# A graph-attention layer on one core: node logits added and weights turned by TensorE, five tiles of every batch fetched by columns

## The chip, the cores and the metric

The kernel runs on one core of one Trainium2 chip. The metric is the device time of one execution in microseconds (us). The profile of one execution is read beside it. Engines are named as in the profile: PE is TensorE, PEld its weight loads, DVE is VectorE, ACT is ScalarE, POOL is GpSimd and SP is SyncE.

## The reference: what is computed

12500 nodes have 128 features, 412500 edges (sorted by target) have 64. Node rows are normalised, cut at zero and projected; every edge gets a logit for each of 4 heads, a leaky step, a softmax over the edges of its target, and the weighted source rows are summed for each target. Cut to what matters:

```python
h = jnp.maximum(_layernorm(x), 0.0)
h = (h @ W_node.T).reshape(num_nodes, H, HD)            # H = 4 heads, HD = 32
e = (edge_attr_64 @ W_edge.T).reshape(num_edges, H, HD)
att = jnp.sum(jnp.concatenate([h[src], h[tgt], e], -1) * a, -1)
att = jnp.where(att > 0, att, 0.2 * att)
m = jnp.maximum(segment_max(att, tgt), 0.0)
ex = jnp.exp(att - m[tgt])
denom = segment_sum(ex, tgt) + (num_edges - deg)[:, None] * jnp.exp(-m)
out = x + segment_sum((ex / denom[tgt])[:, :, None] * h[src], tgt)
```

## The kernel before

A lead-in of some 300 us writes a table of projected node rows (576 B each) to HBM and keeps the normalised node features, turned, in SBUF as `features`. Then come 66 batches. A batch holds 7 chunks of 7 tiles of 128 edges, so 49 tiles; its source rows stand in one of three buffers `hs` (RING = 3).

**Three ways a tile of source rows arrives.** Most tiles come by one indirect gather on POOL each (`gather_tile`, L334). One tile comes row by row, by single DMAs of SP (`row_by_row`, L864). A few tiles come by columns: the 128 source numbers are loaded as registers, 32 at a time, and 32 copies of one column of `features` each (128x1) put them side by side in `turned`; PE projects the tile with the weights `wall` and ACT copies it into `hs` (`put_back`, L904/L905). Such a set of one register load (L852) and 32 copies is called a group here; a tile is four groups. Before, the batches take three and four tiles by columns in turn, and the ones with three also a quarter of the tile that comes by rows (L909/L911), so 13 and 16 groups.

**Who does the groups.** `OF_SCALAR` and `OF_VECTOR` say how many groups ACT (L885) and DVE (L883) do in a batch, of even and of odd number; the batch whose tiles they prepare is two ahead or more. `BEHIND` lists the places in DVE's program where one group may stand; a batch uses the first few of the list. ACT does two groups at fixed places among the work after the exponentials, two more where a merge stands, and what is left of its number at the end of the batch, ahead of the next exponentials.

**A batch b, in program order** (`weigh`, `mark`, `scatter`, `choose`, `close`). The order is written out by hand; each engine goes through its own list in that order.
- POOL: a memset `gate` (L819) waits for the last matmul that reads the buffer to be filled (`scatter` of batch b - 2, L1095), then the gathers of batch b + 1 follow.
- SP: the rows of batch b + 2 with its edge features `eft` between them (L760).
- DVE: `weigh` copies the source logits out of `hs` (L1000), turns them in 32x32 blocks (L1001), adds them to PE's logits `z` in four steps (L1004), does the leaky step (L1007, L1008), two scans for the maximum of each target (L1009, L1012) and a subtraction (L1014). ACT takes the exponential in four steps (L1016), DVE masks the maxima in four (L1018), turns both in one instruction into PSUM (L1021) and copies the maxima into `hs` (L1026). `mark` builds the one-hot matrices `hot` (L951 to L958), `scatter` multiplies the rows by their weights in two pieces (L1089), and PE sums them with 14 matmuls into `pa` (L1095). They may start when ACT has copied the sums of the batch before out of `pa` (`collect`, L1120).
- After that DVE compares targets (`choose`, L789), every second batch DVE and ACT merge two batches' sums into `acc`, and PE begins the logits of batch b + 2 (`begin`, L935 and L938).

Of the kernel before, what the change touches and what calls it, by code (L numbers as in the profile page):

```python
# [9 lines left out]
F32 = mybir.dt.float32  # L10
# [13 lines left out]
H = 4  # L24
# [135 lines left out]
def kernel(  # L160
# [195 lines left out]
    with (  # L356
# [140 lines left out]
        def of_vector(u):  # L497
            return (u.s.b0 + u.i0) // XS % 3 == 0 and u.m == XS
# [228 lines left out]
    bank = ps.tile([P, 2 * T * R + W + GB * 4], F32, name="exr")  # L727
    both_ps = bank[:, :2 * T * R].rearrange("p (w t r) -> p w t r", w=2, t=T)
    ex_ps = both_ps[:, 0, :, :]
    rows_ps = bank[:, 2 * T * R:2 * T * R + W]  # L730
# [252 lines left out]
    def open_weights(s):  # L983

        s.zst = work.tile([P, T, R], F32, name="zst")
# [3 lines left out]
        s.both = work.tile([P, 2, T, R], F32, name="both")  # L989

    def weigh_part(s, t0, t1):

        zst, att, up, m, both = s.zst, s.att, s.up, s.m, s.both
# [3 lines left out]
        def grouped(what, g):  # L997
            return what.rearrange("r (t g i) -> r g t i", g=NQT, i=R)[:, g, t0:t1, :]
# [9 lines left out]
        on_half(s, nc.vector.tensor_tensor(z, up[:, e0:e1], att[:, e0:e1], op=OP.max))  # L1008
# [3 lines left out]
        nc.vector.tensor_tensor_scan(mp[:, ::-1], s.pen[:, e1:e0:-1], up[:, e0:e1][:, ::-1], 0.0, op0=OP.add, op1=OP.max)  # L1012
        of_vector("down")
        on_half(s, nc.vector.tensor_tensor(att[:, e0:e1], z, mp, op=OP.subtract))  # L1014
        for g in range(NQT):
            nc.scalar.activation(both[g * R:(g + 1) * R, 0, t0:t1, :], grouped(att, g), AF.Exp)  # L1016
        for g in range(NQT):
            nc.vector.scalar_tensor_tensor(both[g * R:(g + 1) * R, 1, t0:t1, :], grouped(s.pen[:, 1:], g), -1.0 / BIG,  # L1018
                                           grouped(up, g), op0=OP.mult, op1=OP.mult)
        if t1 - t0 == T:  # L1020
            nc.vector.transpose(both_ps.rearrange("p w t r -> p (w t r)"), both.rearrange("p w t r -> p (w t r)"))  # L1021
        else:
            for w in range(2):
                nc.vector.transpose(both_ps[:, w, t0:t1, :].rearrange("p t r -> p (t r)"),  # L1024
                                    both[:, w, t0:t1, :].rearrange("p t r -> p (t r)"))
        nc.vector.tensor_copy(own, both_ps[:, 1, t0:t1, :s.chunks * H].rearrange("p t (q h) -> p t q h", h=H))  # L1026

# [279 lines left out]
    with tc.manual_schedule():  # L1307
# [20 lines left out]
        for b in range(NBT - 1):  # L1328
# [28 lines left out]
            if later:  # L1357
                put_back(later, 0)
            if b < NBT - 2:
                mark(s)  # L1360
            for store in stores:
# [340 lines left out]
```

## Time and profile before

| what | value |
|---|---|
| time, median of 3 runs | 6768.51 us (6765.73 to 6787.56) |
| the profiled execution: its own time, its span | 6719.83 us, 6718.1 us |
| PE, PEld busy | 1803.4 us (27%), 724.3 us (11%) |
| DVE busy | 2718.8 us (40%), 13514 instructions |
| ACT busy | 2583.9 us (38%), 20492 instructions |
| POOL busy | 2797.8 us (42%), 3018 instructions |
| gathers from the table | 2887, 947 ns each |
| column copies on ACT, on DVE | 18624 (187 ns), 9888 (142 ns) |

No engine is busy for half of the span. Register loads and waits count as idle time, so a group costs more than its copies' busy time; idle time with the word "issue" is time in which an engine waited for nothing that the profile shows.

### The profile page before, as it was taken

How to read it: one execution, taken by the hardware profiler on the slowest of the kernel's cores; microseconds unless marked ns; L12 is line 12 of the kernel's file. 1: busy time of each engine (PE TensorE's matmuls, PEld its weight loads, DVE VectorE, ACT ScalarE, POOL GpSimd, SP SyncE). 2: the span in 40 equal slices, each digit the busy share in tenths (PEclk: the TensorE clock that was granted, in tenths of full speed). 3: DMA queues.
4: the chain of work that ended last, by engine and by line, in shares of the span. 5: the costliest groups of instructions: out<-in, count | busy, mean ns of one | idle time of the engine just before them, and what ended most of it. 6: DMA issues, size and time to landing. Idle time of an engine off the chain costs nothing. (4 is left out here: it accounts for less than half of the span.)

```text
span 6718.1 us, 65140 instructions
## 1 busy us (share of the span) xinstructions
PE 1803.4 (27%) x4569; PEld 724.3 (11%) x4569; DVE 2718.8 (40%) x13514; ACT 2583.9 (38%) x20492; POOL 2797.8 (42%) x3018
## 2 busy tenths in 40 slices
PE   4223123223123232222232232133123223312323
PEld 3101001011011011010011011011011001101111
DVE  4434334344344243353343344344334334434445
ACT  4134334334344344344344344344334434433420
POOL 4453443343443443533533443443453353344351
PEclk8566566566566566665666566566566566656666
DMA  4322222222222222222222222222222222222221
GB/s 115 94 61 58 61 61 64 61 61 62 57 63 65 59 64 60 64 65 57 64 66 61 65 66 61 62 63 61 67 64 65 59 61 67 62 66 65 64 66 43
DMA packets 225620, 432.22 MB, mean 64 GB/s; under 512 B 92316, under 2 KB 125094, under 8 KB 225144
## 3 DMA queue, kind: packets, MB, share of 16 engines
q0 software_dynamic: 94240, 216.84, 13.5%
q1 hardware_dynamic: 100664, 145.09, 7.4%
q10 hardware_dynamic: 30240, 66.08, 2.8%
q14 instruction: 438, 3.59, 0.2%
q8 instruction: 38, 0.62, 0.0%
HBM read 412.21 MB, written 15.53 MB: 64 GB/s over the span
## 5 line engine op out<-in xcount | busy, mean ns | idle before, releaser
L885 ACT COPY turned<-features 128x1 f32 x18624 | 2053.1, 187 | 3473.0 <-issue 3469.9
L334 POOL DMA_INDIRECT hs<-table,ends x2887 | 2734.6, 947 | 1006.8 <-issue 895.0
L819 POOL MEMSET gate<- 128x1 f32 x63 | 6.2, 99 | 2758.7 <-PE pa L1095 2751.6
L1095 PE MATMUL pa<-hs,hot 128*128 128x504 f32 x1820 | 937.0, 680 | 531.5 <-ACT r L1120 478.6
L904 PE MATMUL more<-wall,turned 128*128 128x144 f32 x430 | 155.5, 457 | 3011.5 <-ACT hs L905 2985.0
L883 DVE COPY turned<-features 128x1 f32 x9888 | 681.8, 142 | 691.9 <-issue 689.8
L1021 DVE STREAM_TRANSPOSE exr<-both 128x448 f32<-128x448 f32 x65 | 42.9, 660 | 1530.4 <-ACT both L1016 1529.8
L1095 PEld LDWEIGHTS pa<-hs,hot 128*128 128x128 f32 x1820 | 398.5, 223 | 1045.4 <-issue 505.2
L1089 DVE TENSOR_TENSOR hs<-hs,exr 128x1848 f32<-128x1848 f32 (+1 forms) x130 | 456.6, 3515 | 0.0
L904 PEld LDWEIGHTS more<-wall,turned 128*128 128x128 f32 x430 | 91.5, 265 | 3093.8 <-ACT hs L905 3027.1
L938 PE MATMUL z<-eft,wa 128*32 128x512 f32 (+1 forms) x792 | 354.4, 592 | 61.5 <-DMA eft<-in_ef 61.4
L935 PE MATMUL z<-eft,wa 128*64 128x512 f32 (+1 forms) x132 | 85.6, 738 | 960.1 <-DMA eft<-in_ef 814.5
L1014 DVE TENSOR_TENSOR a<-z,a 32x896 f32<-32x896 f32 (+1 forms) x67 | 71.7, 1070 | 643.5 <-issue 643.3
L1120 ACT COPY r<-pa 32x70 f32<-32x70 f32 (+1 forms) x1040 | 263.6, 253 | 119.3 <-PE pa L1095 88.2
L1004 DVE TENSOR_TENSOR up<-z,zst 32x224 f32<-32x224 f32 (+2 forms) x268 | 104.3, 389 | 429.8 <-PE z L795 418.9
L795 PE MATMUL z<-near_dst,near_rows 128*32 128x512 f32 (+1 forms) x528 | 214.7, 550 | 30.5 <-DVE run L1154 22.6
L1018 DVE SCALAR_TENSOR_TENSOR both<-pen_sb,up 32x224 f32<-32x224 f32 (+2 forms) x268 | 100.3, 374 | 202.2 <-issue 201.7
L1016 ACT ACTIVATE both<-a 32x224 f32<-32x224 f32 (+2 forms) x268 | 102.8, 384 | 172.1 <-DVE a L1014 126.1
L789 DVE TENSOR_TENSOR near_dst<-near_dst,least 128x1792 f32<-128x1792 int32 x66 | 132.4, 2006 | 20.3 <-DMA near_dst<-in_dstc 20.3
L958 DVE TENSOR_TENSOR hot<-exr,key 128x1568 f32<-128x1568 f32 x65 | 116.4, 1791 | 59.3 <-PE pa L1095 57.1
L1009 DVE TENSOR_TENSOR_SCAN up<-pen_sb,z 32x896 f32<-32x896 f32 (+1 forms) x67 | 133.6, 1994 | 2.3
L1194 DVE TENSOR_TENSOR acc<-acc,up 128x70 f32 x461 | 105.1, 228 | 70.7 <-issue 48.6
(203 smaller groups left out, 1503.4 us busy)
## 6 DMA issues: line engine op xcount, KB each, us to landing
hs<-table SPq DMA_DIRECT2D x7072, 0.6 KB
eft<-in_ef SPq DMA_DIRECT2D x231, 448.0 KB
near_dst<-in_dstc ACTq DMA_DIRECT2D x128, 448.0 KB
hs<-table,ends POOLq DMA_INDIRECT x2887
near_rows<-near SPq DMA_DIRECT2D x461, 0.5 KB
pen_sb<-pens SPq DMA_DIRECT2D x66, 98.1 KB
xg<-in_xh SPq DMA_DIRECT2D x13, 448.0 KB
out<-xg SPq DMA_DIRECT2D x13, 448.0 KB
```

The source lines that it names most:

```text
L334: load = nc.gpsimd.indirect_dma_start(out=rows, out_offset=None, in_=of[:, :], in_offset=bass.IndirectOffsetOnAxis(ap=at, axis=0), engine_ ...
L789: nc.vector.tensor_tensor(hot, s.near_dst.bitcast(I32), least[:, s.b, :, None].to_broadcast([P, 2, CE]), op=OP.is_equal)
L795: s.made = own_half(s, nc.tensor.matmul(s.z[:, part], near_rows[:, s.b % 2, k, :], hot[:, k, part], start=False, stop=(k == 1), skip_group ...
L883: nc.vector.tensor_copy(s.turned[:, i:i + 1], column)
L885: nc.scalar.copy(s.turned[:, i:i + 1], column)
L904: nc.tensor.matmul(back_ps, s.turned[:, i * P:(i + 1) * P], wall, start=True, stop=True)
L938: s.made = own_half(s, nc.tensor.matmul(s.z[:, part], wa3[:, j + s.b % 2 * (SB + 1), :], s.eft[:, j, part], start=False, stop=(j == NEXT - ...
L958: nc.vector.tensor_tensor(s.hot.rearrange("p t q r -> p (t q) r"), rows_ps[:, None, :].to_broadcast([P, T * CB, W]), key[:, :, None].to_br ...
L1009: on_half(s, nc.vector.tensor_tensor_scan(up[:, e0:e1], s.pen[:, e0:e1], z, 0.0, op0=OP.add, op1=OP.max))
L1089: nc.vector.tensor_tensor(rows, rows, ex_ps[:, t0:t1, :CB * H, None].to_broadcast([P, t1 - t0, CB * H, HB]), op=OP.mult)
L1095: scattered[s.b] = nc.tensor.matmul(wide_ps[:, g, :], s.hot[:, t, g * NEXT:g * NEXT + SB, :].rearrange("p q r -> p (q r)"), flat[:, at:at ...
L1120: nc.scalar.copy(r[h * W:(h + 1) * W, q:q + NEXT * len(of) - NEXT + 1:NEXT, :], block)
```

## The change

The source logits are no longer turned and added by DVE: seven matmuls against the identity add them to `z` in PSUM, and the leaky step reads `z`. The exponential and the mask are one instruction each over 32x896, and seven PE transposes bring weights and maxima into PSUM (in another order of its columns). `mark` stands ahead of the copy of the maxima now. `scatter` multiplies in three pieces (2, 2 and 3 tiles). From batch 4 to 62 every batch takes five tiles by columns, the even ones a quarter of the tile by rows besides, so 20 and 21 groups: ten on DVE, 11 or 10 on ACT. The list of places has four more. Counted over the whole program, POOL issues 92 gathers fewer, ACT does 61 groups more and DVE 307, PE has 1016 matmuls more (92 of them project the added tiles, whose results ACT copies), and ACT has 201 exponentials fewer.

```diff
-TURNED = 4
-OF_SCALAR = (10, 9)
-OF_VECTOR = (5, 5)
-BEHIND = ("rows", "first", "near", "hot", "down", "up")
+TURNED = 5
+OF_SCALAR = (11, 10)
+OF_VECTOR = (10, 10)
+BEHIND = ("rows", "first", "near", "middle", "hot", "own", "down", "up", "leaky", "end")
...
-    return [(T - 1, CB - TURNED + k) for k in range(TURNED if NEXT < b <= ALL + 3 and b % 2 else TURNED - 1)]
+    return [(T - 1, CB - TURNED + k) for k in range(TURNED if NEXT < b <= ALL + 3 else TURNED - 1)]
...
         nc.vector.tensor_copy(logits[:, t0:t1, :s.chunks * H].rearrange("p t (q h) -> p t q h", h=H), own)
-        nc.vector.transpose(zst[:, t0:t1, :].rearrange("p t i -> p (t i)"),
-                            logits[:, t0:t1, :].rearrange("p t i -> p (t i)"))
-        for g in range(NQT):
-            on_half(s, nc.vector.tensor_tensor(grouped(up, g), grouped(s.z, g),
-                                               zst[g * R:(g + 1) * R, t0:t1, :], op=OP.add))
+        for t in range(t0, t1):
+            s.made = own_half(s, nc.tensor.matmul(s.z[:, t * P:(t + 1) * P], logits[:, t, :], ident,
+                                                  start=False, stop=True, skip_group_check=True))
+        of_vector("own")
         z = s.z[:, e0:e1]
-        nc.vector.tensor_scalar(att[:, e0:e1], up[:, e0:e1], 0.2, None, op0=OP.mult)
-        on_half(s, nc.vector.tensor_tensor(z, up[:, e0:e1], att[:, e0:e1], op=OP.max))
+        on_half(s, nc.vector.tensor_scalar(att[:, e0:e1], z, 0.2, None, op0=OP.mult))
+        on_half(s, nc.vector.tensor_tensor(z, z, att[:, e0:e1], op=OP.max))
+        of_vector("leaky")
...
-        for g in range(NQT):
-            nc.scalar.activation(both[g * R:(g + 1) * R, 0, t0:t1, :], grouped(att, g), AF.Exp)
-        for g in range(NQT):
-            nc.vector.scalar_tensor_tensor(both[g * R:(g + 1) * R, 1, t0:t1, :], grouped(s.pen[:, 1:], g), -1.0 / BIG,
-                                           grouped(up, g), op0=OP.mult, op1=OP.mult)
-        if t1 - t0 == T:
-            nc.vector.transpose(both_ps.rearrange("p w t r -> p (w t r)"), both.rearrange("p w t r -> p (w t r)"))
...
+        nc.scalar.activation(both[:R, e0:e1], att[:, e0:e1], AF.Exp)
+        nc.vector.scalar_tensor_tensor(both[R:, e0:e1], s.pen[:, e0 + 1:e1 + 1], -1.0 / BIG, up[:, e0:e1],
+                                       op0=OP.mult, op1=OP.mult)
+        for t in range(t0, t1):
+            nc.tensor.transpose(both_ps[:, t, :, :].rearrange("p w r -> p (w r)"), both[:, t * P:(t + 1) * P],
+                                ident[:2 * R, :2 * R])
+        if s.b < NBT - 2:
+            mark(s)
...
-        for t0, t1 in ((0, FIRST), (FIRST, T)):
+        for t0, t1 in ((0, FIRST), (FIRST, 2 * FIRST), (2 * FIRST, T)):
...
-            of_vector("rows" if t1 == T else "first")
+            of_vector("rows" if t1 == T else "middle" if t0 else "first")
...
                 put_back(later, 3)
+                put_back(later, 4)
...
+            of_vector("end")
             of_scalar(spare[ENG.Activation])
```

How the change moves instructions is seen at three places. First DVE from the last merge step to the subtraction ahead of the exponentials, before:

```order
L1194 TENSOR_TENSOR acc<-acc,up 128x70 x7
L971 MEMSET hs 128x16x2
L1000 COPY logits<-hs 128x7x28
L1001 STREAM_TRANSPOSE zst<-logits 128x224
L1004 TENSOR_TENSOR up<-z,zst 32x7x32 x4
L1007 TENSOR_SCALAR a<-up 32x896
L1008 TENSOR_TENSOR z<-up,a 32x896
L1009 SCALAR_TENSOR_TENSOR up<-pen_sb,z 32x896
L1012 SCALAR_TENSOR_TENSOR a<-pen_sb,up 32x896
L852 TENSOR_LOAD numbers
L883 COPY turned<-features 128x1 x32
L1014 TENSOR_TENSOR a<-z,a 32x896
```

And in the changed kernel, from the logits copy on (the group of "end" stands just ahead of it):

```order
L996 COPY logits<-hs 128x7x28
L852 TENSOR_LOAD numbers
L883 COPY turned<-features 128x1 x32
L1002 TENSOR_SCALAR a<-z 32x896
L1003 TENSOR_TENSOR z<-z,a 32x896
L852 TENSOR_LOAD numbers
L883 COPY turned<-features 128x1 x32
L1005 SCALAR_TENSOR_TENSOR up<-pen_sb,z 32x896
L852 TENSOR_LOAD numbers
L883 COPY turned<-features 128x1 x32
L1008 SCALAR_TENSOR_TENSOR a<-pen_sb,up 32x896
```

One group stood between the logits copy and the subtraction; now there are four ("own", "leaky", "up" and "down", whose copies follow the last row), and a fifth ahead of the copy.

The second place is PE between the logits of batch b + 2 and the sums of batch b + 1, before:

```order
L935 MATMUL z<-eft,wa_84 64x512
L938 MATMUL z<-eft,wa_84 32x512 x3
L935 MATMUL z<-eft,wa_84 64x384
L938 MATMUL z<-eft,wa_84 32x384 x3
L904 MATMUL more<-wall,turned 128x144 x4
L1095 MATMUL pa<-hs,hot 128x504 x14
```

And in the changed kernel:

```order
L938 MATMUL z<-eft,wa_84 32x384 x3
L998 MATMUL z<-ident,logits 32x128 x7
L1015 MATMUL exr<-ident,both 128x64 x7
L904 MATMUL more<-wall,turned 128x144 x5
L1088 MATMUL pa<-hs,hot 128x504 x14
```

The logits of batch b + 1 (L998) now stand behind the beginning of batch b + 2, and the projections for ACT (L904) behind the transposes of the weights (L1015).

The third place is ACT from the exponentials to the copies out of `pa`, before, in a batch with three tiles by columns:

```order
L1016 ACTIVATE both<-a 32x224 x4
L905 COPY hs<-more 128x144
L780 DMA near_dst<-in_dstc 128x1x896 x2
L905 COPY hs<-more 128x144
L852 TENSOR_LOAD numbers
L885 COPY turned<-features 128x1 x32
L905 COPY hs<-more 128x144
L1120 COPY r<-pa 32x35 x2
```

And in the changed kernel:

```order
L1011 ACTIVATE both<-a 32x896
L905 COPY hs<-more 128x144
L780 DMA near_dst<-in_dstc 128x1x896 x2
L905 COPY hs<-more 128x144
L852 TENSOR_LOAD numbers
L885 COPY turned<-features 128x1 x32
L905 COPY hs<-more 128x144 x3
L1113 COPY r<-pa 32x35 x2
```

Three copies of projected tiles stand behind that group where one stood (two where four tiles came by columns), and the other added group of ACT stands among those ahead of the next exponentials.

More of the change, by code (lines that the diff above doesn't have):

```diff
@@ L727 @@
     bank = ps.tile([P, 2 * T * R + W + GB * 4], F32, name="exr")
-    both_ps = bank[:, :2 * T * R].rearrange("p (w t r) -> p w t r", w=2, t=T)
-    ex_ps = both_ps[:, 0, :, :]
+    both_ps = bank[:, :2 * T * R].rearrange("p (t w r) -> p t w r", w=2, t=T)
+    ex_ps = both_ps[:, :, 0, :]
     rows_ps = bank[:, 2 * T * R:2 * T * R + W]
@@ L983, in open_weights @@
     def open_weights(s):
-        s.zst = work.tile([P, T, R], F32, name="zst")
         a = work.tile([P, BUF], F32, name="a")
@@ L988, in open_weights @@
         s.up = ps.tile([P, BANKS * 512], F32, name="up")[:R, :CE]
[L989 removed]
+        s.both = work.tile([2 * R, CE], F32, name="both")
     def weigh_part(s, t0, t1):
[L993 removed]
+        att, up, m, both = s.att, s.up, s.m, s.both
         own = s.hs.rearrange("p (t q) (h k) -> p t q h k", t=T, h=H)[:, t0:t1, :s.chunks, :, AW - 1]
         e0, e1 = t0 * P, t1 * P
[L997 to L998 removed]
         nc.vector.tensor_copy(logits[:, t0:t1, :s.chunks * H].rearrange("p t (q h) -> p t q h", h=H), own)
[L1001 to L1005 removed]
+        for t in range(t0, t1):
+            s.made = own_half(s, nc.tensor.matmul(s.z[:, t * P:(t + 1) * P], logits[:, t, :], ident,
+                                                  start=False, stop=True, skip_group_check=True))
+        of_vector("own")
         z = s.z[:, e0:e1]
[L1007 to L1008 removed]
+        on_half(s, nc.vector.tensor_scalar(att[:, e0:e1], z, 0.2, None, op0=OP.mult))
+        on_half(s, nc.vector.tensor_tensor(z, z, att[:, e0:e1], op=OP.max))
+        of_vector("leaky")
         on_half(s, nc.vector.tensor_tensor_scan(up[:, e0:e1], s.pen[:, e0:e1], z, 0.0, op0=OP.add, op1=OP.max))
@@ L1014, in weigh_part @@
         on_half(s, nc.vector.tensor_tensor(att[:, e0:e1], z, mp, op=OP.subtract))
-        for g in range(NQT):
-            nc.scalar.activation(both[g * R:(g + 1) * R, 0, t0:t1, :], grouped(att, g), AF.Exp)
-        for g in range(NQT):
-            nc.vector.scalar_tensor_tensor(both[g * R:(g + 1) * R, 1, t0:t1, :], grouped(s.pen[:, 1:], g), -1.0 / BIG,
-                                           grouped(up, g), op0=OP.mult, op1=OP.mult)
-        if t1 - t0 == T:
[L1021 to L1026, printed above, removed]
+        nc.scalar.activation(both[:R, e0:e1], att[:, e0:e1], AF.Exp)
[6 more added lines that the diff above has]
+            mark(s)
+        nc.vector.tensor_copy(own, both_ps[:, t0:t1, 1, :s.chunks * H].rearrange("p t (q h) -> p t q h", h=H))
     spans = ((0, EARLY), (EARLY, T))
@@ L1358 @@
                 put_back(later, 0)
-            if b < NBT - 2:
-                mark(s)
             for store in stores:
```

## The prediction, made before the changed kernel ran

> **What bounds the kernel now.** I read the busy times first, then the costliest groups, then the timelines of POOL, ACT, DVE and PE over one pair of batches in the middle. No busy time explains the span:
>
> ```profile
> PE 1803.4 (27%) x4569; PEld 724.3 (11%) x4569; DVE 2718.8 (40%) x13514; ACT 2583.9 (38%) x20492; POOL 2797.8 (42%) x3018
> ```
>
> Behind them stand groups of instructions (line, engine, what, count; busy time, mean of one; idle time before them and who ended it):
>
> ```profile
> L885 ACT COPY turned<-features 128x1 f32 x18624 | 2053.1, 187 | 3473.0 <-issue 3469.9
> L334 POOL DMA_INDIRECT hs<-table,ends x2887 | 2734.6, 947 | 1006.8 <-issue 895.0
> L819 POOL MEMSET gate<- 128x1 f32 x63 | 6.2, 99 | 2758.7 <-PE pa L1095 2751.6
> L883 DVE COPY turned<-features 128x1 f32 x9888 | 681.8, 142 | 691.9 <-issue 689.8
> L1021 DVE STREAM_TRANSPOSE exr<-both 128x448 f32<-128x448 f32 x65 | 42.9, 660 | 1530.4 <-ACT both L1016 1529.8
> ```
>
> ACT's column copies hold it for 2053.1 + 3473.0 = 5526 us of 6718. POOL stands 2758.7 us at its gate, for PE's sums; DVE waits 1529.8 us for ACT's exponentials. So POOL waits for PE, PE for ACT, and ACT is never short of work. When its copies are slow is seen on POOL's and ACT's timelines (start, duration, line, count, idle before):
>
> ```profile
> 3395.02 0.10 POOL L819 MEMSET gate<- 128x1 f32 x1 [40.76 <-PE pa L1095]
> 3395.88 0.94 POOL L334 DMA_INDIRECT hs<-table,ends  x1 [0.76 <-issue]
> ...
> 3449.94 0.94 POOL L334 DMA_INDIRECT hs<-table,ends  x1 [0.30 <-issue]
> 3495.28 0.10 POOL L819 MEMSET gate<- 128x1 f32 x1 [44.40 <-PE pa L1095]
> ...
> 3593.10 0.10 POOL L819 MEMSET gate<- 128x1 f32 x1 [39.86 <-PE pa L1095]
> ```
>
> Gate to gate is a batch: 100.26 and 97.82 us. Its 44 gathers fill 3395.88 to 3450.88, so 1.25 us each.
>
> ```profile
> 3394.08 3.06 ACT L885 COPY turned<-features 128x1 f32 x32 [0.95 <-issue]
> ...
> 3400.07 2.49 ACT L885 COPY turned<-features 128x1 f32 x25 [1.82 <-issue]
> ...
> 3440.25 0.19 ACT L885 COPY turned<-features 128x1 f32 x1 [1.21 <-issue]
> ...
> 3457.05 0.19 ACT L885 COPY turned<-features 128x1 f32 x1 [0.51 <-issue]
> 3457.76 2.32 ACT L885 COPY turned<-features 128x1 f32 x24 [0.51 <-issue]
> 3461.02 2.60 ACT L885 COPY turned<-features 128x1 f32 x27 [0.94 <-issue]
> 3463.52 0.56 ACT L885 COPY turned<-features 128x1 f32 x5
> ...
> 3464.78 0.79 ACT L1016 ACTIVATE both<-a 32x224 f32<-32x224 f32 x2
> 3465.59 0.28 ACT L905 COPY hs<-more 128x144 f32<-128x144 f32 x1
> 3466.81 0.28 ACT L905 COPY hs<-more 128x144 f32<-128x144 f32 x1 [0.94 <-PE more L904]
> ```
>
> A group takes 3.06 + 0.95 = 4.0 us outside the gathers. Soon after they begin, and until 6 us after the last, ACT gets one copy in 0.19 + 1.21 = 1.40 us: a table of stretches (from and to, length, busy time of this line on ACT with its copies, clock, DMA share, GB/s) has
>
> ```profile
> 3402.50:3457.00 54.50, 8.47 (x47) 0.60 0.23 56
> ```
>
> 47 copies in 54.5 us. Then the 56 that are left run fast, the exponentials follow at once and end at 3465.57, 70.6 us after the gate. DVE has the same two paces (its timeline, same columns):
>
> ```profile
> 3396.20 1.80 DVE L1194 TENSOR_TENSOR acc<-acc,up 128x70 f32 x7 [1.51 <-issue]
> ...
> 3407.28 1.10 DVE L1008 TENSOR_TENSOR z<-up,a 32x896 f32<-32x896 f32 x1
> ...
> 3410.49 2.01 DVE L1012 TENSOR_TENSOR_SCAN a<-pen_sb,up 32x896 f32<-32x896 f32 x1
> 3412.69 1.37 DVE L883 COPY turned<-features 128x1 f32 x21 [0.19 <-issue]
> ...
> 3427.66 0.15 DVE L883 COPY turned<-features 128x1 f32 x1 [1.25 <-issue]
> 3438.86 1.09 DVE L1014 TENSOR_TENSOR a<-z,a 32x896 f32<-32x896 f32 x1 [11.05 <-issue]
> ...
> 3469.43 2.03 DVE L883 COPY turned<-features 128x1 f32 x32 [0.41 <-issue]
> ```
>
> Some 30 instructions, 21 copies among them, pass at full speed after the stage has begun, then one in 1.40 us, and a step that waits for the last copy comes 11 us late. That makes some 30 + 54.5 / 1.40 = 69 in a stage, 65 with a wait or two. Outside, a group costs 2.0 us behind a step as long as its load. The rest of a batch is on PE:
>
> ```profile
> 3407.78 0.51 PE L904 MATMUL more<-wall,turned 128*128 128x144 f32 x2
> 3465.92 0.85 PE L904 MATMUL more<-wall,turned 128*128 128x144 f32 x2 [57.63 <-ACT hs L905]
> ...
> 3481.38 13.78 PE L1095 MATMUL pa<-hs,hot 128*128 128x504 f32 x28 [8.21 <-ACT r L1120]
> ```
>
> The sums wait for ACT's copies out of `pa`, 8.21 us after DVE's first product, and take 13.8. So a batch is a sum of stages, one behind the other: gathers (55) and their tail (6 to 7), what ACT has left until the exponentials end (8), ACT's way from there to the sums (16), the sums (14), the gate (1). What lies in the gather stage is free until its 47 copies on ACT, or those 65 instructions on DVE, are used up; what is over pays at full speed behind it.
>
> **The change part by part**, for the pair; A is the batch of 100.26 us (ten groups on ACT, a merge in it), B the one of 97.82.
>
> *Gathers.* A goes from 44 to 43, B from 45 to 43: -1.25 and -2.5 us. SP's list keeps its length: the same rows, and the source numbers come as six rows of one DMA instead of four or five.
>
> *One more group on ACT.* The slow stage holds no more copies than before, so its 32 copies come behind it: +4.0 in each.
>
> The load of 32 registers has its own row:
>
> ```profile
> L852 ACTq TENSOR_LOAD <-numbers x582: 1943/1967/2907, 321.5 to 6444.6; - x194
> ```
>
> It takes 1.97 us, of which 0.95 shows between groups. The Trainium skill, "Runtime: NRT & Kernel Launch", section "Instruction fetch mechanics", gives a load about 200 ns for each register even in bulk. By that a group would take some 6.4 + 3.06 us, an estimate, and this term 9.5 instead of 4.0; the row does not agree, with 61 ns.
>
> *Five more groups on DVE.* Those of "middle", "hot" and "end" cost 2.0 us where ACT or PE is awaited anyway; should that cover go, they add 6. The four between the logits copy and the subtraction count. In A, DVE comes out of the merge at 3396.20 + 1.80, 3.0 us after the gate (the longer way of ACT moves its exponentials of the merge as well), with the groups "end" and "own" still to do. Its 65 instructions end inside "own"; behind the stage follow half a group (0.9), the leaky step (1.1 + 1.1), a load's rest (1.0), three groups (6.0), two scans (4.1) and the subtraction (1.1): 15.3 us. ACT's own rest is 3457.76 to 3463.99, 6.2, and 4.0 more: 10.2. So DVE ends last in A, by up to 5.1 us; zero if it is quicker out of the merge. I take 4.0, nearer to the count: A pays 4.0 + 4.0. In B nothing is merged, "end" and "own" are over before the stage, and 65 instructions hold the leaky step, its group, a scan and 29 copies of "up". DVE has left the others (0.2), a scan (2.1), a group (2.0) and the subtraction (1.1), 5.4 us. ACT's own rest is there
>
> ```profile
> 3560.54 0.93 ACT L885 COPY turned<-features 128x1 f32 x9 [0.51 <-issue]
> ...
> 3561.38 0.56 ACT L885 COPY turned<-features 128x1 f32 x5
> ```
>
> 1.3 us, and 4.0 more: 5.3, as good as a tie, +0.2. Ends for DVE's share: 0 and, with the wait of 11 us behind the last copy, 11 in one batch of the pair.
>
> *One exponential.* Four took 1.58 us; one over 32x896 costs at least one of the four (0.39) and at most all: I take 1.0, so -0.55 in each. The single mask, the lost transposes (0.66 for the one of 128x448) and the four additions are DVE work off the path (its first product is 8.21 us early).
>
> *PE's transposes.* They are new between the exponentials and ACT's first copy of a projected tile, whose matmul ran 58 us ahead (3407.78) and now comes behind. The nearest transposes are those of the lead-in:
>
> ```profile
> 92.58 0.49 PE L516 MATMUL pt<-ident,hn 128*128 128x128 f32 x3
> ```
>
> and, over all of them,
>
> ```profile
> L516 PE MATMUL pt<-ident,hn 128*128 128x128 f32 x156 | 32.7, 320 | 6.4 <-DVE hn L510 3.0 <-ACT hn L507 1.7 <-issue 1.0
> ```
>
> Seven at 0.32 are 2.2, the projection behind them takes 0.85 in a PE that has rested (3465.92): +3.1, the value that I take, since PE rests there too. At the 0.16 of a quick PE it is 2.0, the low end; all of it hidden is a rival. The five projections and ACT's whole list behind them wait with it. The seven matmuls of the logits stand behind the beginning of batch b + 2, in the stage under the gathers: nothing, as long as `eft` is there.
>
> *Added tiles.* Each copy costs ACT 0.94 + 0.28 = 1.2 us ahead of the sums: one in A, two in B: +1.2 and +2.4.
>
> *Late `eft`.* In the first third SP brings `eft` late; waits for ACT's projected tiles sum to
>
> ```profile
> ACT hs L905 <- PE more L904: 137.5, 90, 8.8
> ```
>
> 90 x 0.94 = 85 are the usual ones, so about 53 us are such delays. Longer batches give SP time at its quick pace: -50 in all (0 and -53 as ends).
>
> The sum: A -1.25 + 8.0 - 0.55 + 3.1 + 1.2 = +10.5; B -2.5 + 4.2 - 0.55 + 3.1 + 2.4 = +6.65; +17.15 a pair. Batches 4 to 61 are 29 pairs: +497, with the 50 +447, 6720 + 447 = 7167 in the profiled execution's terms. Its own time is 0.7% under the median of the runs, so x 6768.5/6719.8: **7220 us**. All low ends (one exponential at 0.39, no share of DVE's, 2.0 for the transposes: +9.5 a pair) give 6990; DVE's 11 us in one batch of each pair, with nothing won at the exponential and at `eft`, gives 7510.
>
> **The rivals.**
> *Fewer gathers carry it (faster).* The Trainium skill, "Perfetto Trace Analysis", section "Identifying the Most-Contended Engine", says to optimise the engine with the highest occupancy first. POOL is the busiest engine of the page with 42%, and the change relieves it. As a mechanism here: ACT's and DVE's added groups all find room, the exponentials keep their distance from the last gather, and the stage shrinks: 92 x 1.25 = 115, 62 x 0.55 = 34 and 50 us less, 6570 us. It decides if what is added behind the gathers stays under 1.9 us a batch. The 47 copies in 54.5 us and POOL's 2758.7 us at the gate speak against it. 7%.
> *It cancels (no change).* ACT's group is paid (4.0 a batch), transposes and tiles hide behind DVE's products, DVE keeps up: +1.6 a batch, +95 - 50, about 6810, or nothing. The 8.21 us in which PE waits for ACT alone speak against it. 4%.
> *DVE's waits grow.* Four groups fill its queue, and each step behind a group comes up to 11 us late: 9 us more in every batch, +522, 7750. Against it: the steps that wait run mostly behind the stage. 8%.
> *`eft` stays late.* The logits now stand behind the beginning of the next batch but one; where `eft` lands after the exponentials' old time, DVE's 14 us from the leaky step to the subtraction come on top. Ten such pairs: +140, and no 50 won, 7410. For it: delays up to 8.8 us in the row above. 13%.
>
> **Chances.** The forecast has 68%. Range 6900 to 7500: from a little under the low ends to the high ones, with the late `eft` in it; the two cheap cases and DVE's growing waits (19%) are left out. A measurement here can tell about 0.3%: faster 7%, same 4%, slower 89%.
>
> **What would show it.** After: gathers of 43 in a row; ACT's exponentials 68 to 78 us after the gate; in merging batches DVE's wait for ACT gone and ACT waiting for the subtraction instead; ACT's first copy of a projected tile 3 us behind the exponential; PE's sums 20 us behind it. Wrong it is if copies in the gather stage keep pace, or if DVE reaches the subtraction before the gathers end.

## The result and the profile after

The changed kernel takes 7231.16 us (median of 4 runs, 7225.56 to 7240.77), the kernel before 6767.12 us beside it: ratio 1.068, 95% interval 1.0656 to 1.0705. A second measurement, later, gave 7212.49 against 6733.64 us, 1.0709 (1.0691 to 1.0727). Forecast were 7220 us.

The page of the profile after, its busy times and the groups that answer to those shown of before:

```profile
PE 2018.3 (28%) x6139; PEld 942.9 (13%) x6139; DVE 3202.8 (44%) x22798; ACT 2754.9 (38%) x22335; POOL 2714.6 (38%) x2926
L885 ACT COPY turned<-features 128x1 f32 x20576 | 2233.0, 187 | 3503.7 <-issue 3488.6
L334 POOL DMA_INDIRECT hs<-table,ends x2795 | 2651.0, 948 | 976.7 <-issue 866.6
L883 DVE COPY turned<-features 128x1 f32 x19712 | 1370.5, 143 | 1772.2 <-issue 1767.3
L819 POOL MEMSET gate<- 128x1 f32 x63 | 6.4, 102 | 3406.8 <-PE pa L1088 3406.8
```

POOL gathers 84 us less than before (2651.0 for 2734.6) and stands 648 us longer at its gate. The waits of ACT's exponentials for DVE's subtraction (total, times, longest), before and after:

```profile
ACT both L1016 <- DVE a L1014: 126.1, 4, 75.1
ACT both L1011 <- DVE a L1010: 312.8, 66, 93.6
```

Before, ACT ran from its last column copy straight into the exponentials, but for four waits at the start, at the end and in one odd batch. Now it waits in every batch, mostly for 1 to 5 us; the long waits are still at the start, at the end and in the odd batch. One merging batch (A) and the one behind it (B), by POOL's gates:

```profile
3405.69 0.10 POOL L819 MEMSET gate<- 128x1 f32 x1 [48.74 <-PE pa L1088]
3517.64 0.10 POOL L819 MEMSET gate<- 128x1 f32 x1 [57.62 <-PE pa L1088]
3623.60 0.10 POOL L819 MEMSET gate<- 128x1 f32 x1 [51.59 <-PE pa L1088]
```

111.95 and 105.96 us, where the pair before took 100.26 and 97.82. ACT's timeline at the end of A's gathers, then of B's (last group, exponential, first copy of a projected tile):

```profile
3477.74 3.06 ACT L885 COPY turned<-features 128x1 f32 x32 [0.94 <-issue]
3482.22 0.95 ACT L1011 ACTIVATE both<-a 32x896 f32<-32x896 f32 x1 [1.42 <-DVE a L1010]
3485.23 0.28 ACT L905 COPY hs<-more 128x144 f32<-128x144 f32 x1 [2.06 <-PE more L904]
...
3581.93 3.06 ACT L885 COPY turned<-features 128x1 f32 x32 [0.94 <-issue]
3588.38 0.95 ACT L1011 ACTIVATE both<-a 32x896 f32<-32x896 f32 x1 [3.39 <-DVE a L1010]
3591.33 0.28 ACT L905 COPY hs<-more 128x144 f32<-128x144 f32 x1 [2.00 <-PE more L904]
```

The exponential stands 76.5 and 70.7 us behind the gate, waits for DVE in both batches, and the next copy comes 2.0 us behind it instead of at once. DVE's timeline over the same pair:

```profile
3431.74 0.50 DVE L996 COPY logits<-hs 128x196 f32<-128x196 f32 x1 [10.11 <-issue]
...
3467.51 1.08 DVE L1002 TENSOR_SCALAR a<-z 32x896 f32<-32x896 f32 x1
...
3481.11 1.08 DVE L1010 TENSOR_TENSOR a<-z,a 32x896 f32<-32x896 f32 x1
...
3512.14 2.04 DVE L883 COPY turned<-features 128x1 f32 x32 [1.72 <-issue]
3551.86 1.08 DVE L1002 TENSOR_SCALAR a<-z 32x896 f32<-32x896 f32 x1 [37.68 <-remote]
...
3579.14 2.02 DVE L1005 TENSOR_TENSOR_SCAN up<-pen_sb,z 32x896 f32<-32x896 f32 x1 [9.00 <-remote]
...
3587.20 1.08 DVE L1010 TENSOR_TENSOR a<-z,a 32x896 f32<-32x896 f32 x1
```

In A the leaky step stands at the end of the gather stage and 14.7 us of steps and groups follow from its start on, near the 15.3 that were forecast. In B it comes 34.2 us behind the gate (in the kernel before at 4.7), and the first scan only behind the stage. PE's timeline shows what released it:

```profile
3503.13 14.39 PE L1088 MATMUL pa<-hs,hot 128*128 128x504 f32 x28 [8.21 <-ACT r L1113]
...
3523.45 0.71 PE L998 MATMUL z<-ident,logits 128*32 128x128 f32 x5
3589.54 0.98 PE L1015 MATMUL exr<-ident,both 64*128 64x64 f32 x7 [65.38 <-DVE both L1012]
```

The last logits matmul ends at 3524.16, 6.5 us behind the gate, when the slow pace has begun; the leaky step runs 27.7 us later. The same kind of sum says that late `eft` has gone from ACT's list: the longest wait for a projected tile was 8.8 us before.

```profile
ACT hs L905 <- PE more L904: 277.5, 210, 2.1
```

### The profile page after: what moved, and what is told of

Same layout as the page of the kernel before. It is cut to its first block, busy times and chain, and to the rows that moved or that the text cites. A ratio compares the mean times of both kernels' runs of the same rounds, so it can differ in the third digit from the quotient of the medians.

```text
span 7233.6 us, 79666 instructions
## 1 busy us (share of the span) xinstructions
PE 2018.3 (28%) x6139; PEld 942.9 (13%) x6139; DVE 3202.8 (44%) x22798; ACT 2754.9 (38%) x22335; POOL 2714.6 (38%) x2926
## 5 line engine op out<-in xcount | busy, mean ns | idle before, releaser
L885 ACT COPY turned<-features 128x1 f32 x20576 | 2233.0, 187 | 3503.7 <-issue 3488.6
L334 POOL DMA_INDIRECT hs<-table,ends x2795 | 2651.0, 948 | 976.7 <-issue 866.6
L883 DVE COPY turned<-features 128x1 f32 x19712 | 1370.5, 143 | 1772.2 <-issue 1767.3
L819 POOL MEMSET gate<- 128x1 f32 x63 | 6.4, 102 | 3406.8 <-PE pa L1088 3406.8
L1015 PE MATMUL exr<-ident,both 64*128 64x64 f32 x462 | 64.7, 315 | 3359.7 <-DVE both L1012 3295.1
L1002 DVE TENSOR_SCALAR a<-z 32x896 f32<-32x896 f32 (+1 forms) x67 | 71.7, 1070 | 1222.7 <-remote 971.4
L1015 PEld LDWEIGHTS exr<-ident,both 64*128 64x128 f32 x462 | 54.1, 215 | 3381.3 <-ACT both L1011 3326.3
L904 PE MATMUL more<-wall,turned 128*128 128x144 f32 x614 | 260.0, 527 | 406.8 <-ACT hs L905 382.0
L998 PE MATMUL z<-ident,logits 128*32 128x128 f32 x924 | 160.0, 344 | 628.7 <-DVE logits L996 467.2
L905 ACT COPY hs<-more 128x144 f32<-128x144 f32 x307 | 85.0, 277 | 356.3 <-PE more L904 277.5
L904 PEld LDWEIGHTS more<-wall,turned 128*128 128x128 f32 x614 | 153.9, 311 | 498.8 <-ACT hs L905 465.7
L998 PEld LDWEIGHTS z<-ident,logits 128*32 128x32 f32 x924 | 122.7, 140 | 664.4 <-DVE logits L996 483.0
L1011 ACT ACTIVATE both<-a 32x896 f32<-32x896 f32 (+1 forms) x67 | 62.8, 937 | 355.1 <-DVE a L1010 312.8
```

The source lines that it names most:

```text
L334: load = nc.gpsimd.indirect_dma_start(out=rows, out_offset=None, in_=of[:, :], in_offset=bass.IndirectOffsetOnAxis(ap=at, axis=0), engine_ ...
L883: nc.vector.tensor_copy(s.turned[:, i:i + 1], column)
L885: nc.scalar.copy(s.turned[:, i:i + 1], column)
L904: nc.tensor.matmul(back_ps, s.turned[:, i * P:(i + 1) * P], wall, start=True, stop=True)
L998: s.made = own_half(s, nc.tensor.matmul(s.z[:, t * P:(t + 1) * P], logits[:, t, :], ident, start=False, stop=True, skip_group_check=True))
L1015: nc.tensor.transpose(both_ps[:, t, :, :].rearrange("p w r -> p (w r)"), both[:, t * P:(t + 1) * P], ident[:2 * R, :2 * R])
```

## The experiments

Times from gate to gate, on POOL's timeline, are the measure in all of them: the mean over 27 merging batches (A) and 28 others (B) from the middle, one odd batch left out.

| kernel | A, us | B, us | ratio to before (95%) |
|---|---|---|---|
| before | 103.8 | 96.3 | 1 |
| changed kernel, first and second measurement | 112.2, 112.1 | 104.6, 104.4 | 1.068, 1.0709 |
| weights alone | 103.4 | 98.3 | 1.0091 (1.0074 to 1.0108) |
| tiles alone | 109.4 | 103.6 | 1.0569 (1.0551 to 1.0587) |
| logits first | 111.7 | 102.5 | 1.0634 (1.0616 to 1.0652) |
| projection first | 109.3 | 102.4 | 1.0522 (1.0504 to 1.0539) |
| one group to DVE | 116.0 | 104.3 | 1.0882 (1.0863 to 1.0902) |
| fewer tiles | 118.5 | 84.6 | 1.0172 (1.0155 to 1.0189) |
| still fewer | 116.8 | 85.5 | 1.0125 (1.0108 to 1.0141) |
| half rows | 92.1 | 84.1 | 0.8858 (0.8842 to 0.8873) |
| one tile, half rows | 88.9 | 85.4 | 0.8770 (0.8754 to 0.8786) |
| half rows, new weights | 94.1 | 89.3 | 0.9199 (0.9182 to 0.9217) |

The kernel before took 6720 to 6767 us beside all of these. Before's A holds some ten batches of 109 to 112 us with late `eft`; from the 26th batch on the pair is 101.6 and 96.6.

**The weights alone and the tiles alone.** The first is the changed kernel with the numbers of before, the second the kernel before with the places and numbers of the change.

```diff
 weights alone, against the changed kernel
-TURNED = 5        OF_SCALAR = (11, 10)   OF_VECTOR = (10, 10)   BEHIND = (... ten places)
+TURNED = 4        OF_SCALAR = (10, 9)    OF_VECTOR = (5, 5)     BEHIND = (... six places, as before)
-... range(TURNED if NEXT < b <= ALL + 3 else TURNED - 1)
+... range(TURNED if NEXT < b <= ALL + 3 and b % 2 else TURNED - 1)
-                put_back(later, 4)

 tiles alone, against the kernel before: these numbers the other way round, and
+        of_vector("own")                 (ahead of the leaky step)
+        of_vector("leaky")               (behind it)
-        for t0, t1 in ((0, FIRST), (FIRST, T)):
+        for t0, t1 in ((0, FIRST), (FIRST, 2 * FIRST), (2 * FIRST, T)):
+            of_vector("rows" if t1 == T else "middle" if t0 else "first")
+            of_vector("end")
+                put_back(later, 4)
```

> Only the new way of the weights (logits added and weights turned by PE, one exponential); four tiles by columns, groups 10 and 9 on ACT, 5 on DVE, as before. Theory 'columns' (the moved tile's groups are the loss): here only -0.6 us for the exponential and +2 to +3 us for the seven transposes ahead of ACT's first projected tile remain, +1.5 to +2.5 us a batch, minus some of the late eft: 6800 to 6930 us, ratio 1.005 to 1.025. Rival 'chain' (the additions on PE and their wait on DVE are the loss): most of the 464 us is there without the tiles, over 7050 us, ratio over 1.04.

> Only the tiles: five by columns in every batch, groups 11 and 10 on ACT and 10 on DVE at the same places, on the weights of before (additions and transposes on DVE, four exponentials). 'Columns': per pair ACT's group twice +8.0, DVE's excess +4, copies of added tiles +3.6, gathers -3.75: +12 a pair, 29 pairs +349, minus up to 50 for the late eft: 7040 to 7130 us, ratio 1.04 to 1.055. 'Chain': under 6930 us, ratio under 1.025.

6777.11 and 7103.27 us, against 6719.86 on the same chip: 0.9% and 5.7%. The first lies inside what "columns" said, the second a little above it (1.0569 for 1.04 to 1.055), and far from "chain" both; together (1.0091 x 1.0569 = 1.0665) they make nearly the whole of 1.068 to 1.071. The loss is the moved tiles. In the weights alone the way behind the exponential shows the transposes' price (ACT's timeline):

```profile
3348.87 0.94 ACT L1011 ACTIVATE both<-a 32x896 f32<-32x896 f32 x1
3351.68 0.28 ACT L905 COPY hs<-more 128x144 f32<-128x144 f32 x1 [1.87 <-PE more L904]
```

The copy waits 1.87 us, and PE's sums start 17.3 us behind the exponential in B, where they started at 14.6. DVE's leaky step comes late in B here too (25.8 us behind the gate on average, before 4.7), but with five groups on DVE the subtraction still ends 7 us ahead of ACT's last copy: without the added groups this lateness costs nothing.

**The logits first.**

```diff
             s.made = own_half(s, nc.tensor.matmul(s.z[:, t * P:(t + 1) * P], logits[:, t, :], ident, ...
+        if 1 <= s.b < NBT - 2:
+            begin(batch(s.b + 1))
         of_vector("own")
...
-            if b + 2 < NBT:
+            if b + 2 == NBT - 1:
                 begin(batch(b + 2))
```

> The changed kernel, with PE's seven logits matmuls ahead of the first matmuls of the next batch instead of behind them: 2 to 4 us earlier on PE. Theory 'late release': in batches without a merge DVE's leaky step is let go 6.6 us after the gate, when the gathers already hold DVE's sequencer, and so comes 34 us after the gate instead of 4.7; ACT then waits 1.1 or 3.4 us for the subtraction. Let go 3 to 4 us after the gate the step runs there, the wait in those batches goes, the merging batches stay: -1 to -2.3 us in 31 batches, 7160 to 7200 us, ratio to the changed kernel 0.990 to 0.996. Rival 'count' (the number of DVE's instructions, not when the step is let go, sets the subtraction): 7231, no change.

B falls by 1.9 us and ACT's wait there is gone; A stays. PE, DVE and ACT of a B batch whose gate stands at 3464.10:

```profile
3466.94 1.36 PE L998 MATMUL z<-ident,logits 128*32 128x128 f32 x11
...
3472.21 1.08 DVE L1004 TENSOR_SCALAR a<-z 32x896 f32<-32x896 f32 x1 [11.90 <-remote]
...
3529.98 1.08 DVE L1012 TENSOR_TENSOR a<-z,a 32x896 f32<-32x896 f32 x1
...
3531.16 0.95 ACT L1013 ACTIVATE both<-a 32x896 f32<-32x896 f32 x1
```

Let go 2.0 us earlier against the gate (the last logits matmul ends 4.5 us behind it instead of 6.5), the leaky step runs 8.1 us behind the gate instead of 34.2, and ACT goes from its copies into the exponential. 7141.45 us, ratio 1.0634: under both measurements of the changed kernel, by 0.4 and 0.7%. "Late release" holds, at the upper part of what it said; "count" does not.

**The projection first.**

```diff
+        if s.b + 2 < NBT:
+            put_back(batch(s.b + 2), 0)
         for t in range(t0, t1):
             nc.tensor.transpose(both_ps[:, t, :, :] ...
...
             if later:
-                put_back(later, 0)
```

> The changed kernel, with PE's first projection of a tile by columns ahead of the seven transposes, as before the change. If the transposes delay ACT's list behind the exponential, ACT's first copy of a projected tile follows the exponential at once instead of 2.06 us later, the second one 1.6 us earlier (a DMA that ACT issues between them takes 1.7), PE's sums start 1.6 us earlier: 62 x 1.6 = 100, 7130 us, ratio to the changed kernel 0.986. If DVE's products hold the sums anyway (they end 16.6 us behind the exponential, the sums start at 19.9): no change, 7231.

```profile
3403.50 0.95 ACT L1011 ACTIVATE both<-a 32x896 f32<-32x896 f32 x1 [3.87 <-DVE a L1010]
...
3404.48 0.28 ACT L905 COPY hs<-more 128x144 f32<-128x144 f32 x1
...
3422.28 14.54 PE L1090 MATMUL pa<-hs,hot 128*128 128x504 f32 x28 [8.20 <-ACT r L1115]
```

The copy follows at once, the sums start 17.8 us behind the exponential's end instead of 19.9, A and B fall by 2.8 and 2.0: 7070.51 us, 1.0522, a little more than expected. The order on PE was a price of its own, and the cheapest part to get back.

**One group to DVE.**

```diff
-OF_SCALAR = (11, 10)   OF_VECTOR = (10, 10)
+OF_SCALAR = (10, 9)    OF_VECTOR = (11, 11)
             of_vector("end")
+            of_vector("last")
```

> The changed kernel, with one of ACT's groups moved to DVE: 10 and 9 on ACT, 11 and 11 on DVE, the new one at the end of the batch behind the one that stands there. Theory 'the sum counts' (both engines are full, and DVE already ends last): in merging batches DVE reaches the subtraction 2.0 us later and ACT's 4.0 us less only lengthen its wait; in the others nothing is won, since ACT waits 1.1 to 3.4 us for DVE there already: +2.0 in 31 batches, ratio to the kernel before 1.07 to 1.08. Rival 'ACT alone' (each of its groups costs 4.0 in each batch, wherever DVE stands): -4.0 x 62, ratio 1.025 to 1.04.

DVE's and ACT's timeline in a merging batch (gate at 3443):

```profile
3504.21 0.50 DVE L996 COPY logits<-hs 128x196 f32<-128x196 f32 x1 [3.74 <-DVEq L314]
...
3523.21 0.95 ACT L1011 ACTIVATE both<-a 32x896 f32<-32x896 f32 x1 [10.21 <-DVE a L1010]
```

ACT's copies end 3.5 (A) and 3.6 us (B) sooner than in the changed kernel on the same chip, and it waits 10.2 us here. B is unchanged, as "the sum counts" said; A grows by 3.9, twice as much, since the added copies push the logits copy itself out of the gather stage (61.6 us behind the gate, in the changed kernel 21 to 37). 1.0882, above the 1.07 to 1.08 expected: DVE has no room for the moved group in A, and in B ACT's shorter list only waits longer.

**Fewer tiles.** If the groups are the loss, taking some from the kernel before should win. Two groups of ACT that stood between the exponentials and the last copy of the sums go as well.

```diff
-TURNED = 4        OF_SCALAR = (10, 9)
+TURNED = 3        OF_SCALAR = (6, 5)       (still fewer: TURNED = 2, OF_SCALAR = (2, 1))
-            if k == SB // 2:
-                of_scalar()
...
-            of_scalar()
```

> The kernel before, turned the other way: three and two tiles by columns instead of four and three, 6 and 5 groups on ACT instead of 10 and 9 (5 on DVE as before), and none of ACT's groups between the exponentials and the last copy of the sums (two stood there). Gathers rise by one a batch. 'Columns' (what lies over the free copies of the gather stage pays 4.0 us a group): four groups less on ACT are worth up to 16 us a batch, the gather costs 1.25; the exponentials move into the gather stage, PE's sums follow the last gather by a few us: 82 to 92 us a batch, 5700 to 6250 us, ratio 0.85 to 0.93. Rival 'POOL' (the gathers set the time, and ACT's copies are filler beside them): +1.25 x 62 = +78, ratio 1.01. Rival 'freed and lost' (the exponentials and what follows creep at one instruction in 1.40 us until the gathers end, and nothing is won over what the two groups behind the exponentials held): ratio 0.95 to 1.0.

> The same with two and one tiles by columns, 2 and 1 groups on ACT, 5 on DVE, one gather more a batch. If ACT's groups no longer set anything at 6 and 5, only the gather is left: +1.25 x 62 = +78 us over the run with three and two tiles (ratio to before up 0.01). If they still do, up to 16 us a batch less: ratio to before under 0.85.

6846.97 and 6817.28 us, 1.0172 and 1.0125: the forecast gain did not come, and neither of the two outcomes named for still fewer did. The time is near what "POOL" gave, but its mechanism is not in the trace: B fell to 84.6 us, and A rose to 118.5. POOL's gates around one A, SP's timeline, PE's and ACT's in it, and the sum of PE's wait:

```profile
3590.02 0.10 POOL L819 MEMSET gate<- 128x1 f32 x1 [25.68 <-PE pa L1095]
3710.86 0.10 POOL L819 MEMSET gate<- 128x1 f32 x1 [64.11 <-PE pa L1095]
...
3627.38 33.28 SPq L864 DMA_DIRECT2D hs<-table  x32
...
3663.30 10.62 SPq L864 DMA_DIRECT2D hs<-table  x32
3673.97 0.84 SPq L760 DMA_DIRECT2D eft<-in_ef  x2
...
3678.52 1.97 PE L935 MATMUL z<-eft,wa 128*64 128x512 f32 x2 [85.41 <-DMA eft<-in_ef]
...
3688.55 0.28 ACT L905 COPY hs<-more 128x144 f32<-128x144 f32 x1 [26.45 <-PE more L904]
...
PE z L935 <- DMA eft<-in_ef: 2521.3, 32, 85.9
```

SP hardly rests: 32 rows take 10.6 us outside the gathers, and the pieces of `eft` stand between them. PE waits 85 us for one. The exponentials of that batch had run at 3660.52, behind ACT's own copies; but PE's projections stand behind the late logits, so ACT's first copy of a projected tile waits 26.45 us, and the sums with it. The trace points at SP's list as what bounds the kernel as soon as ACT has less to do; the next run tests it.

**Half the rows.** If so, halving SP's rows at about the same number of groups must bring the gain that fewer tiles did not.

```diff
-    return 0 if not rows_of(b) else P - GROUP if turned_of(b) and b % 2 == 0 else P
+    return 0 if not rows_of(b) else P // 2 if turned_of(b) else P
-TURNED = 4   OF_SCALAR = (10, 9)   ... range(TURNED if NEXT < b <= ALL + 3 and b % 2 else TURNED - 1)
+TURNED = 2   OF_SCALAR = (5, 5)    ... range(TURNED)        (one tile: TURNED = 1, OF_SCALAR = (1, 1))
 (and, as in fewer tiles, no group of ACT behind the exponentials)
```

> Two tiles by columns in every batch, and of the tile that SP brings row by row only 64 rows (before 96 or 128), the other 64 by columns: ten groups, 5 on ACT and 5 on DVE (fewer_tiles had 10.5), one gather or none more than there. Theory 'SP next': with fewer tiles the batch became short enough that SP's list of rows (2 instructions a row, 0.32 us a row outside the gathers, 2.8 us in them) could no longer be worked off, eft came late and the merging batches took 116 to 121 us instead of the 92.6 of the one that had it in time, the others 84 to 90. With half the rows eft is in time: 92.6 and 85 us, 62 x 88.8 + the 510 outside = 6015 us, ratio to before 0.88 to 0.93. Rival 'not SP' (eft is late since the gathers hold the DMA queues, or the sums wait for something else): the merging batches stay at 116 to 121, ratio 1.0 to 1.02.

> The same with one tile by columns, six groups: 1 on ACT, 5 on DVE, one gather more. If neither ACT nor SP sets the end there: +1.25 x 62 = +78 us over half_rows, ratio up 0.012. If ACT's groups still cost there (4.0 us each behind the gathers): a lower ratio than half_rows, by up to 0.03.

PE's wait for `eft`, and a wait of SP's rows that fewer tiles did not have:

```profile
PE z L935 <- DMA eft<-in_ef: 53.5, 2, 47.0
SPq L864 <- PE pa L1095: 190.6, 46, 14.2
```

5954.14 us (0.8858), A at 92.1 and B at 84.1, close to the 92.6 and 85 that were put together from single batches. `eft` is in time, and SP now waits for others: "SP next" is shown. With one tile 5893.53 us (0.8770): A wins 3.2 more, B pays its gather with 1.3. Both beat the kernel before beside them by 11 and 12%, on the one chip where this was measured.

**Half rows with the new weights.** The numbers of half rows, in the changed kernel:

```diff
-TURNED = 5   OF_SCALAR = (11, 10)   OF_VECTOR = (10, 10)   BEHIND = (... ten places)
+TURNED = 2   OF_SCALAR = (5, 5)     OF_VECTOR = (5, 5)     BEHIND = (... six places, as before)
+... P // 2 if turned_of(b) else P      (and no group of ACT behind the exponential)
```

> half_rows on the changed kernel's weights (logits added and weights turned by PE, one exponential). Where the exponentials stand in or right behind the gathers, an instruction on DVE or ACT costs 1.40 us until they end: the new weights have 3 exponentials and 8 DVE instructions less in that stretch, against 2.1 us for the transposes ahead of ACT's list. If DVE's count sets the merging batches: 8 x 1.4 = 11 us less in these where they still wait for the subtraction, ratio 0.03 to 0.05 below half_rows. If the transposes and PE's wait decide: up to 2.6 us a batch more, ratio up to 0.025 above it.

6184.48 us (0.9199), 0.034 above half rows. The second half of that expectation (transposes and PE's wait) had the sign right and the price too small. The late release is back: in a batch B of DVE's timeline, with its gate at 2849.05, the leaky step waits 35.7 us:

```profile
2884.54 1.08 DVE L1002 TENSOR_SCALAR a<-z 32x896 f32<-32x896 f32 x1 [35.70 <-remote]
```

The additions of half rows start 3 us behind the gate there. The exponentials of that batch come 66.7 us behind the gate, instead of 31 to 35 in half rows, so that products and sums stand behind the gathers with all that they need: B takes 89.3 us instead of 84.1. This is read from the trace; no run put the logits first here.

**All gathered.**

```diff
-SINGLE = 2
+SINGLE = NBT
```

> The kernel before with all 49 tiles of a batch gathered by POOL: no tile by columns, none row by row by SP. In one_tile_half_rows the batches without a merge have their exponentials 32 us after the gate, and then DVE's 32 copies of the group 'hot' creep until the gathers end and hold the products: 85.4 us a batch. Theory 'instructions' (in the gathers an engine gets one instruction in 1.40 us, and what counts is how many a batch has): without copies DVE's some 50, ACT's some 27 and SP's some 30 instructions fit beside 49 gathers (61.3 us), products and sums run in the gather stage too, the gate hardly waits: 64 to 80 us a batch, 62 x 72 + 510 = 4970 us, ratio to before 0.70 to 0.83. Rival 'behind the gathers' (products and sums need the stage's end anyway, 8 + 15.4 us behind it): 61.3 + 1 + 24 = 87 us a batch and two gathers more than in one_tile_half_rows, ratio 0.88 to 0.92.

4266.30 us, ratio 1.0646 (1.0629 to 1.0664) - but beside it the kernel before took 4008.31 us (4002.52 to 4009.12, 7 runs), where it had taken 6720 to 6767 on the other chips. The expectation's premise did not hold on this chip. POOL and DVE in the middle of the gathers, the one wait at the gate that is left, and POOL's group:

```profile
2005.92 0.95 POOL L334 DMA_INDIRECT hs<-table,ends  x1 [0.30 <-issue]
2006.86 0.12 POOL L819 MEMSET gate<- 128x1 f32 x1
2007.17 0.95 POOL L334 DMA_INDIRECT hs<-table,ends  x1 [0.19 <-issue]
...
2014.49 1.68 DVE L1004 TENSOR_TENSOR up<-z,zst 32x224 f32<-32x224 f32 x4
2016.20 1.08 DVE L1007 TENSOR_SCALAR a<-up 32x896 f32<-32x896 f32 x1
...
POOL gate L819 <- PE pa L1095: 13.1, 1, 13.1
...
L334 POOL DMA_INDIRECT hs<-table,ends x3165 | 3081.9, 974 | 1055.7 <-issue 899.6
```

DVE's steps follow one another without the pace of 1.40 us although gathers run, and POOL goes from batch to batch without a wait: 64.0 us each for 49 gathers. That the chip makes this difference, and not the missing copies and rows, rests on the time of the kernel before beside it, of which there is no trace there. Why this kernel is the slower one on that chip was only argued: it has 278 gathers more than before (3165 for 2887; 278 x 1.25 = 347 us, measured 258). For the question that it was run for it decides nothing. Whether the changed kernel, with 92 gathers less than before, would be the faster one on such a chip (92 x 1.25 = 115 us of 4008, if POOL alone sets the time there) was not measured, nor were the half rows.

## Why the prediction was right, and where it was off

By its own steps, means of the batches from the 26th on, where `eft` is in time on both sides:

- *Gathers:* 43 in a row in both kinds of batches, the last one 1.2 and 2.4 us earlier. Right.
- *The slow pace:* the 47 copies in 54.5 us from which it was read make 1.16 us each, not 1.40. Most copies stand 1.40 us apart, some 0.70 or less. ACT's term went by the 47, so it did not suffer; DVE's 65 instructions were counted with 1.40.
- *ACT's group:* +4.0 us a batch. In B ACT's copies end 67.3 us behind the gate, 5.7 behind the stage (5.3 forecast); taking one group away moved that by 3.5 to 3.6. Right, if a little large.
- *DVE's excess:* right in A (exponential's end 77.7 us behind the gate for 71.4: +6.3, forecast -1.25 + 8.0 - 0.55 = +6.2), though by its sum more than by its split: ACT's own copies end 4.7 us later in the first trace and 3.2 in the second (2.75 forecast), and ACT then waits 2.2 and 3.3 us for DVE (4.0 forecast). Wrong in B: forecast +1.15, measured +3.2 (70.6 for 67.4). The failed step is the sentence that costs the logits' seven matmuls at "nothing, as long as `eft` is there". Behind `begin` they end 6.5 us behind the gate, too late for DVE to pass the leaky step before the slow pace, and in the batch shown both scans and two groups were left over instead of one of each. Logits first gave 1.9 us a batch back, nearly all of the miss. In tiles alone, without the matmuls, ACT waits for DVE in B too, by 2 to 4 us. DVE's timeline there, in a batch whose gate stands at 3242.88, shows another premise failing, that "own" is over before the stage:

```profile
3245.92 1.65 DVE L1004 TENSOR_TENSOR up<-z,zst 32x224 f32<-32x224 f32 x4 [6.45 <-PE z L795]
3249.39 1.63 DVE L883 COPY turned<-features 128x1 f32 x24 [1.82 <-issue]
...
3259.32 1.08 DVE L1008 TENSOR_SCALAR a<-up 32x896 f32<-32x896 f32 x1 [0.56 <-issue]
```

DVE's additions wait for PE and end 4.7 us behind the gate, so the copies of "own" come 6.5 us behind it: 24 of them pass fast, eight creep, and the leaky step follows 16.4 us behind the gate.

- *One exponential:* 0.95 for 1.58, -0.63; forecast -0.55.
- *Transposes:* forecast +3.1 by a slow PE. Seven took 0.98 instead of 2.2, and with the projection behind them ACT's copy came 2.0 us late, the low end. By the sums' start it was more: 2.7 in the weights alone, and projection first gave 2.0 us of it back. No run separates the rest; the size was nearly right, its reason was not.
- *Added tiles with them:* sums 19.9 us behind the exponential, for 15.8 and 14.6: +4.1 and +5.3, forecast +4.3 and +5.5. In tiles alone the sums start 17.0 behind it: +1.2 and +2.4 for the tiles, as forecast. Right.
- *Late `eft`:* -50 forecast. 31 pairs at +18.5 would be 574 us; the 62 batches grew by 518, so 56 came back. Right.
- *The sum:* +17.15 a pair forecast, +18.5 measured (+10.6, +7.9); with 31 pairs instead of 29 it should have read 532, not 497. The two traces differ by 515 us, the forecast had 447: 68 too little. The scale from the profiled execution to the median (x 1.0072, +52) then covered most of that. It had no ground: the kernel before took 6720 us in its profile and in another measurement, 6767 beside the changed kernel, so the 0.7% lie between chips or occasions, and the profile after stands at its own median. That 7220 came so near is luck: two errors of opposite sign. Without them the sum still gives the direction and 447 of the 515.
- *What would show it:* exponentials 68 to 78 us behind the gate, ACT waiting for DVE, sums 20 behind: seen. ACT waits in both kinds of batches, not in A alone, and its first copy comes 2 us behind the exponential, not 3.

The rivals: that fewer gathers carry it is out on these chips, by POOL's gate; on the one chip without the slow pace it may be so, which was not measured. The rule of the Trainium skill, "Perfetto Trace Analysis", section "Identifying the Most-Contended Engine", points at POOL. The trace of all gathered agrees for that chip (no wait at the gate but 13.1 us); the traces of the kernel before and of the changed one, with POOL at its gate for 2758.7 and 3406.8 us, do not; half rows had 91 gathers more than the kernel before (2978 for 2887) and took 11% less time. That it cancels is out by the time: transposes and tiles did not hide. That DVE's waits grow happened in a smaller form: 2 us in B, not 9 in every batch. `eft` did not stay late: after the start no batch but the odd one stands out.

## What to carry to other kernels

A stage in which other engines get an instruction only now and then is a budget: count instructions, not microseconds, and look at what is released after it has begun, since a step that becomes ready 2 us later there can run 26 us later. Before moving work between engines ask which list is full next: here ACT, DVE and SP were all nearly full, one or two more tiles a batch on ACT and DVE cost 6%, and taking work from ACT alone won nothing until SP's list was cut too, then it won 11 to 12% on the one chip where that was measured. And run the kernel before beside every experiment, on more than one chip: what bounds it may be the chip's and not the kernel's.

## What the runs showed of the hardware

- The slow pace beside indirect gathers (most often an instruction in 1.40 us on ACT and DVE, a row of SP's in two of them) was there in the traces of all other measurements and absent in the last: the same kernel took 6720 to 6767 us and 4008 us. What differs between these chips no run here shows, and the trace of the kernel before on the fast one is missing.
- A step that waits for another engine and is let go inside the stage can start late by some 20 times this pace: 27.7 us in the changed kernel, where the same step let go 2.0 us sooner started 3.6 us after PE was done. In the weights alone it was 19 us in B and 36 in A, on average. Why it is so long no run here shows.
- Seven PE transposes of 64x128 took 0.98 us on a PE that had rested 65 us, less than half of what the lead-in's transposes suggested.
